# A written order for VectorE, ScalarE and GpSimd in an attention stage, with norms split in three, two widths of buffers and a later set-up

## The chip, the cores and the metric

The kernel runs on one core of one Trainium2 chip. The metric is the time of one execution on the device, in microseconds (us). Before the change three executions took 1590.54, 1592.66 and 1595.66 us; their median is 1592.66 us.

A core has these engines, each with an instruction queue of its own that is worked off in order: TensorE (PE in the profile; the loading of its weights is shown as PEld), VectorE (DVE), ScalarE (ACT), GpSimd (POOL) and SyncE (SP), which here only issues DMAs.

## The reference

The input is 32 sequences of 256 rows of 128 numbers. Two blocks follow each other, each as x = x + norm(block(norm(x))).

- The first block is a decoder layer: self-attention with a causal mask, cross-attention to one encoder sequence of 256 rows (the same for all 32), with an additive logit per key and a mask that lets a query see two keys past its own place, and an MLP with 512 hidden units and gelu. A layer norm stands ahead of each of the three, and a residual sum behind. There are 16 heads of 8 numbers.
- The second block is a mixture of experts: a shared expert and 8 routed ones of which the gate takes two, each a gated silu unit with 128 hidden units.

```python
q, k, v = split(layer_norm(h) @ c_attn_w + c_attn_b)
h = h + attend(q, k, v, causal) @ attn_proj_w + attn_proj_b
q = layer_norm(h) @ q_attn_w + q_attn_b
h = h + attend(q, k_enc, v_enc, scorer_logits, mask) @ x_proj_w + x_proj_b
h = h + gelu(layer_norm(h) @ fc_w + fc_b) @ mlp_proj_w + mlp_proj_b
x = x + norm(h)
x = x + norm(shared(norm(x)) + sum of two experts chosen per row)
```

## The kernel before, in words

**Stages.** The program has three stages: attention (lines 200 to 676), MLP with the choice of experts (lines 786 to 899), experts (lines 904 to 990). The change touches the first alone.

**One attention.** An object of class `Attention` is one sequence's self-attention (called S0 to S31 here) or cross-attention (X0 to X31). Its work is cut into pieces:

- `load` (line 350) brings 256 rows of x into one of five buffers. `normed_in` (line 361) takes means and variances on VectorE (`moments`, line 176), the power -1/2 on GpSimd (`rsqrt`, line 186: a `tensor_scalar` and a `pow` each), and writes normed rows on VectorE (`normed`, line 194). For a self-attention it does so twice: `xn`, which feeds the queries and keys, and `h_all`, the residual.
- `turned` (382) transposes `xn` on TensorE; `projections` (387) makes queries and keys, which ScalarE moves out of PSUM and GpSimd splits into three bf16 parts with four instructions (`projected`, lines 250 to 253: `qkp`). SP writes the parts to DRAM and reads them back in another layout (`load_queries`, line 262; `load_keys`, line 266). `values` (404) does the same for the values, without the detour.
- `maxima` (420) makes scores with queries on the partitions, and VectorE takes the row maxima, straight from PSUM (line 443). `split` (446) cuts these into three parts on GpSimd with five small instructions (`mparts`), `turned_maxima` (457) transposes them.
- `weights` (477) makes the scores once more with keys on the partitions, less the maxima, and ScalarE takes the exponential into SBUF buffers `wt` from the pool `wtp`, 22 buffers of 512 numbers (lines 502, 503).
- `weighted` (513) multiplies the weights with the values, for each half of the queries (line 525), ScalarE copies the result (`avs`). `back`, `turned_back` and `joined` (536 to 567) divide by the sums on VectorE, transpose and project, and VectorE adds to the residual.

**PSUM.** All that TensorE writes goes to 8 banks of 512 numbers, shared by all pieces (`bank`, line 161). A bank is free again when VectorE or ScalarE has read it.

**The order.** A planner (lines 584 to 649) gives each piece a step. Two steps make one pass of the loop at line 664. A pass issues the matmuls of up to two halves of maxima and two of weights, mixed (`issue`, line 569), then the reductions or exponentials that read them (`after`), and then the other pieces due at the two steps, `weighted` last. One self-attention takes 6 steps of maxima and one cross-attention 8, so from about step 96 on one sequence takes 14 steps, which is 7 passes.

The loop stands in a `manual_schedule` for TensorE (line 662): TensorE gets its instructions in the order of the program. For the other engines the framework's scheduler makes the order at build time, by its own estimate of durations, and it may move an instruction ahead as far as buffers allow. SP's order comes from it too, before the change and after it.

A norm is due 18 steps ahead of an attention's first scores, `turned` 14 steps ahead and `projections` 2 steps after that; a planner's budget may move them by 2.

**Set-up.** Constants are made by pieces of their own: `spares` and `diagonals` fill masks on GpSimd (lines 108 to 132), `max_frames` clears buffers on GpSimd (307), `picks`, `out_biases` and `logit_parts` work on VectorE (134 to 173), and `encoder_turned`, `encoder_rows`, `encoder_keys` and `encoder_values` (315 to 330) prepare the encoder's keys and values, which the first cross-attention uses at step 46. Before the change nearly all of it is due ahead of step 0 (lines 651 to 661).

Of the kernel before, what the change touches and what calls it, by code (L numbers as in the profile page):

```python
# [8 lines left out]
F32 = mybir.dt.float32  # L9
# [6 lines left out]
P = 128  # L16
# [8 lines left out]
EPS = 1e-5  # L25
# [19 lines left out]
def transformer_moe_kernel(ctx: ExitStack, tc: tile.TileContext, ins, out: bass.AP):  # L45
# [130 lines left out]
    def moments(pool, srcs, tag):  # L176

        n = len(srcs)
        st = pool.tile([P, n, 6], F32, tag=f"st{tag}", name="st")
        mv = pool.tile([P, n, 2], F32, tag=f"mv{tag}", name="mv")  # L180
        for i, s in enumerate(srcs):
            nc.vector.bn_stats(st[:, i, :], s)  # L182
            nc.vector.bn_aggr(mv[:, i, :], st[:, i, :])
        return mv

    def rsqrt(pool, mv, mul, add, tag):

        n = mv.shape[1]
        r = pool.tile([P, n], F32, tag=f"r{tag}", name="r")
        nc.gpsimd.tensor_scalar(r, mv[:, :, 1], mul, add, ALU.mult, ALU.add)  # L190
        nc.gpsimd.tensor_tensor(r, r, nhalf[:, 0:n], ALU.pow)  # L191
        return r

    def normed(dst, src, mv, r, i):
        nc.vector.tensor_scalar(dst, src, mv[:, i, 0:1], r[:, i : i + 1], ALU.subtract, ALU.mult)  # L195
# [4 lines left out]
    with ExitStack() as actx:  # L200
        wk = actx.enter_context(tc.tile_pool(name="wk", bufs=3))
        wl = actx.enter_context(tc.tile_pool(name="wl", bufs=5))
        wtp = actx.enter_context(tc.tile_pool(name="wtp", bufs=22))
        kx = actx.enter_context(tc.tile_pool(name="kx", bufs=1))
        dram = actx.enter_context(tc.tile_pool(name="dram", bufs=1, space=bass.MemoryType.DRAM))

# [135 lines left out]
        class Attention:  # L342
# [11 lines left out]
            def spares(self):  # L354
# [3 lines left out]
                if not self.cross:  # L358
                    fill_spare(k_rows[i], k_spare)

            def normed_in(self):
                self.xn = wk.tile([P, 2, D], F32, tag="xn", name="xn")
                if self.cross:
                    mv = moments(wk, self.hs, "a")
                    r = rsqrt(wk, mv, 1.0, EPS, "a")
                    for t in range(2):
                        normed(self.xn[:, t, :], self.hs[t], mv, r, t)
                else:

                    xs = [self.x[:, t, :] for t in range(2)]  # L370
                    mv = moments(wk, xs, "a")
                    r1 = rsqrt(wk, mv, 1.0, EPS, "a")
                    r2 = rsqrt(wk, mv, 1.0 + EPS, EPS * EPS, "b")
                    for t in range(2):
                        normed(self.xn[:, t, :], xs[t], mv, r2, t)
                        normed(self.hs[t], xs[t], mv, r1, t)

            def biased(self):
                h = h_all[:, 2 * self.b : 2 * self.b + 2, :]
# [97 lines left out]
            def weights(self, kb, js, gp):  # L477
                q0, nq = self.queries(kb)
                n = len(js)
                work, tiles = {}, []  # L480
                for g in (2 * gp, 2 * gp + 1):
                    st = slice(32 * g, 32 * g + 32)
                    t = bank("st")[:, 0 : n * nq]
                    t3 = t.rearrange("p (c q) -> p c q", q=nq)
                    tiles.append((g, t))
                    todo = []
                    for c, j in enumerate(js):
                        for part in range(3):
                            todo.append((nq, t3[:, c, :], self.kr[st, j, part, kb * P : kb * P + P],
                                         self.qs[st, j, q0:S], (c, part) == (0, 0)))  # L490
                        todo.append((nq, t3[:, c, :], pick[st, j, :], self.mT[st, q0:S], False))
                    for a in range(4):
                        at = 32 * a - (2 if self.cross and kb == 0 else 0)
                        skip = max(0, -at)
                        w = 32 - skip
                        todo.append((n * w, t3[:, :, at + skip : at + 32], eye[st, a, :],
                                     tri_k[st, skip:32].unsqueeze(1).to_broadcast([32, n, w]), False))
                    work[g] = todo

                def after():  # L500
                    for g, t in tiles:
                        w = wtp.tile([P, 512], F32, tag="wt", name="wt")
                        nc.scalar.activation(w[:, 0 : n * nq], t, AF.Exp)  # L503
                        for c, j in enumerate(js):
                            self.wts[kb, g, j] = w[:, c * nq : (c + 1) * nq]
                    self.done += 1
                    if self.done == len(self.key_halves()):
                        give(("qs", self.cross, self.b % QK_BUFS), self)
                        if not self.cross:
                            give(("kr", self.b % QK_BUFS), self)  # L510
                return work, after
# [75 lines left out]
        def on(step, f, *args):  # L587
            extra.setdefault(step, []).append((f, args))
# [15 lines left out]
        while ended < NB:  # L604
            ready = ended < begun and first[ended] <= at
            cross = begun == NB or (ready and not cross) or begun - ended == AHEAD
            if cross:
                x = pairs[ended][1]
                at = max(at, first[ended])
                ended += 1  # L610
            else:
                x = pairs[begun][0]
                begun += 1

            at = max(at, *(free.get((x.cross, what, x.b % n), at) for what, n in (("qk", QK_BUFS), ("v", V_BUFS))))
            at += at % 2
            halves, keys = x.query_halves(), x.key_halves()
            s = at
            at += len(halves)
            if not x.cross:  # L620
                on(s - 22, x.load)
            on(s - 18, x.normed_in)
            if x.b < QK_BUFS:
                on(s - 17, x.spares)
            on(s + 2, x.biased)
            e = full(s - 14, 0.35, x.turned)
            e = full(e + 2, 0.5 if x.cross else 0.9, x.projections)
            assert e <= s - 8, (e, s)
            if not x.cross:
                full(e + 2, 0.55, x.values)  # L630
            for i, h in enumerate(halves):
                by_query[s + i] = (x, h)
            for qb in range(2):
                last = s + max(i for i, h in enumerate(halves) if h[0] == qb)
                on(last + 1, x.split, qb)
                e = full(last + 3, 0.13, x.turned_maxima, qb)
                assert e < s + LAG
            for i, h in enumerate(keys):
                by_key[s + LAG + i] = (x, h)
            end = s + LAG + len(keys)  # L640
            free[x.cross, "qk", x.b % QK_BUFS] = end + 14
            half = end if x.cross else s + LAG + sum(h[0] == 0 for h in keys)
            e = full(half + 1, 1.2 if x.cross else 0.9, x.weighted, 0)
            e = full(max(e, end + 1), 1.8, x.weighted, 1)
            free[x.cross, "v", x.b % V_BUFS] = e + 12
            e = full(e + 2, 0.5, x.back)
            e = full(e + 2, 0.25, x.turned_back)
            e = full(e + 2, 0.6, x.joined)
            first[x.b] = e + 20

        on(-18, spares)
        on(-15, diagonals)
        on(-13, max_frames, False)
        on(-11, picks)
        on(-9, out_biases)
        full(-5, 0.5, encoder_turned)
        on(-5, logit_parts)
        on(-4, encoder_rows)
        full(-2, 0.5, encoder_keys)
        full(0, 0.5, encoder_values)  # L660
        on(2, max_frames, True)
        with tc.manual_schedule(engines={mybir.EngineType.PE}):
            s = min(extra) // 2 * 2 - 1
            while s <= max(extra):

                works = []
                for t in (s, s + 1):
                    works += [x.maxima(*h) for x, h in [by_query[t]]] if t in by_query else []
                    works += [x.weights(*h) for x, h in [by_key[t]]] if t in by_key else []
                issue(*[w for w, _ in works])  # L670
                for _, after in works:
                    after()
                for f, args in sorted(extra.get(s, []) + extra.get(s + 1, []),
                                      key=lambda e: e[0].__name__ == "weighted"):
                    f(*args)
                s += 2
# [109 lines left out]
    with ExitStack() as mctx:  # L786
        wk = mctx.enter_context(tc.tile_pool(name="wkm", bufs=3))
# [103 lines left out]
        E = mybir.EngineType  # L891
# [149 lines left out]
```

## Time and profile before

| | |
|---|---|
| time, median of three | 1592.66 us |
| time of the profiled execution | 1591.84 us |
| its span, first to last instruction | 1590.1 us |
| mean granted TensorE clock | 0.963 |
| busy: PE, DVE, ACT, POOL | 1407.4, 1054.3, 870.9, 653.1 us |
| attention | 0 to about 1015 us |
| MLP and choice | about 1015 to 1200 us |
| experts | about 1200 to 1590 us |

The span is 1.74 us shorter than the time of that execution. Busy time counts an engine as busy from the start to the end of each instruction; a busy TensorE needn't be at its peak, since matmuls overlap. An idle stretch of an engine is put down to the instruction that ended it: "PE av L525 <- DVE m L443" is TensorE waiting to start line 525, which writes `av`, until a reduction at line 443 was through. "Issue" stands for waits that the profile shows no cause of. PEclk is the share of TensorE's full clock that was granted.

### The profile page before, as it was taken

The numbers are of one execution on the slowest core, as the hardware profiler recorded it, in microseconds if no ns is written. First come the engines' busy times: TensorE is split into PE (matmuls) and PEld (weight loads), VectorE is DVE, ScalarE is ACT, GpSimd is POOL, SyncE is SP. The second block draws the span as 40 slices with busy tenths as digits, with TensorE's granted clock in tenths as the row PEclk, the third lists the DMA queues.
The fourth block names the chain that finished last, engine by engine and source line by source line (L and its number), as shares of the span: only waits on it lengthen the run. The fifth ranks groups of instructions, "written<-read, shape, count | busy, mean of one in ns | idle before, by whom it ended". The sixth has DMA issues, their size and how long they took to land.

```text
span 1590.1 us, 74601 instructions
## 1 busy us (share of the span) xinstructions
PE 1407.4 (89%) x32988; PEld 1099.7 (69%) x32988; DVE 1054.3 (66%) x2955; ACT 870.9 (55%) x2032; POOL 653.1 (41%) x1475
## 2 busy tenths in 40 slices
PE   3678898898988988888999899799979999999997
PEld 2566677776777777777777787478756666666664
DVE  5647667776677776677776666267866666666665
ACT  1353566665666666666666655677734443433433
POOL 7435445444445444444444322378631212222112
PEclk8788999999999999999999989899979999999998
DMA  5632223232232232232222200500000000000000
GB/s 140 189 99 79 65 91 101 65 115 77 71 115 73 91 100 66 84 103 64 93 89 82 66 16 28 148 20 1 1 1 8 7 14 14 8 14 14 7 14 14
DMA packets 106037, 97.27 MB, mean 61 GB/s; under 512 B 4764, under 2 KB 105360, under 8 KB 105712
## 3 DMA queue, kind: packets, MB, share of 16 engines
q1 hardware_dynamic: 104432, 91.49, 18.7%
q8 instruction: 258, 4.23, 1.1%
q10 hardware_dynamic: 1280, 1.01, 0.2%
q14 instruction: 67, 0.55, 0.1%
HBM read 54.47 MB, written 37.77 MB: 58 GB/s over the span
## 4 chain that ended last, share of the span: by engine, by line
PE 66%; DVE 18%; POOL 6%; ACT 4%; issue 3%; DMA 3%; SPq 0%; POOLq 0%; ACTq 0%; DVEq 0%
DVE m L443 11%; PE av L525 11%; PE sc L580 9%; PE po L940 8%; PE pa L929 8%; PE pb L930 8%; PE st L580 7%; PE po L844 4%; PE pf L837 3%; PE pq L245 2%; POOL r L191 2%; ACT wt L503 2%; DVE st L182 2%; PE pa L541 1%; DVE xn L195 1%
## 5 line engine op out<-in xcount | busy, mean ns | idle before, releaser
L443 DVE TENSOR_REDUCE m<-sc 128x2 f32<-128x512 f32 (+2 forms) x896 | 496.2, 607 | 236.8 <-PE sc L580 207.3
L503 ACT ACTIVATE wt<-st 128x512 f32<-128x512 f32 (+1 forms) x896 | 420.7, 539 | 261.1 <-PE st L580 199.8
L580 PEld LDWEIGHTS <-qs 32*128 32x128 bf16 x6144 | 226.4, 95 | 96.7 <-issue 83.5
L580 PE MATMUL st<-mT,pick 32*128 32x256 bf16 (+2 forms) x2048 | 242.7, 245 | 3.8 <-issue 3.7
L580 PEld LDWEIGHTS <-strips 32*128 32x128 bf16 x7424 | 190.2, 94 | 21.8 <-issue 18.4
L940 PEld LDWEIGHTS po<-w,h 128*128 128x128 f32 x1152 | 154.7, 191 | 67.9 <-issue 49.5
L580 PE MATMUL sc<-kr,qs 32*128 32x256 bf16 (+1 forms) x3072 | 165.6, 250 | 33.4 <-DMA kr<-k 24.7
L580 PE MATMUL st<-qs,kr 32*128 32x128 bf16 (+1 forms) x3072 | 179.3, 248 | 8.3 <-issue 4.8
L580 PE MATMUL st<-qs,krx 32*128 32x130 bf16 (+1 forms) x3072 | 177.6, 243 | 7.4 <-issue 5.6
L580 PE MATMUL sc<-krx,qs 32*128 32x256 bf16 (+1 forms) x3072 | 178.9, 246 | 5.6 <-issue 2.6
L934 DVE SCALAR_TENSOR_TENSOR h<-pb,cols,sa 128x512 f32<-128x512 f32 x144 | 107.9, 749 | 113.7 <-ACT sa L932 88.8
L932 ACT ACTIVATE sa<-pa,cols 128x512 f32<-128x512 f32 x144 | 99.7, 693 | 147.3 <-PE pa L929 120.4
L940 PE MATMUL po<-w,h 128*128 128x128 f32 x1152 | 161.9, 277 | 0.0
L929 PE MATMUL pa<-h_all,w 128*128 128x512 f32 x288 | 150.7, 605 | 0.0
L930 PE MATMUL pb<-h_all,w 128*128 128x512 f32 x288 | 147.9, 595 | 0.0
L580 PE MATMUL sc<-strips 32*128 32x64 bf16 (+2 forms) x3840 | 140.2, 193 | 6.5 <-issue 6.4
L580 PE MATMUL st<-strips 32*128 32x64 bf16 (+2 forms) x3584 | 137.2, 193 | 8.7 <-issue 8.6
L954 POOL TENSOR_TENSOR z<-z 128x512 f32<-128x512 f32 x32 | 40.7, 1271 | 245.9 <-ACT z L950 245.9
L525 PE MATMUL av<-wt,vpadx 128*32 128x128 f32 (+1 forms) x4096 | 111.5, 252 | 32.2 <-DVE m L443 28.6
L191 POOL TENSOR_TENSOR r<-r,nhalf 128x2 f32<-128x2 f32 (+1 forms) x160 | 133.0, 837 | 9.9
L580 PEld LDWEIGHTS <-kr 32*128 32x128 bf16 x3072 | 118.1, 95 | 16.7 <-issue 13.9
L525 PEld LDWEIGHTS av<-wt,vpadx 128*32 128x32 f32 x4096 | 97.8, 112 | 44.4 <-DVE m L443 36.6
(162 smaller groups left out, 2649.8 us busy)
## 6 DMA issues: line engine op xcount, KB each, us to landing
kr<-k SPq DMA_DIRECT2D x32, 768.0 KB
k<-qkp SPq DMA_DIRECT2D x32, 576.0 KB
qs<-q SPq DMA_DIRECT2D x64, 256.0 KB
q<-qkp SPq DMA_DIRECT2D x64, 192.0 KB
x<-in_x_dram SPq DMA_DIRECT2D x32, 128.0 KB
x_all<-in_x_dram SPq DMA_DIRECT2D x8, 512.0 KB
out_dram<-y SPq DMA_DIRECT2D x16, 256.0 KB
w<-in_rw_dram SPq DMA_DIRECT2D x1, 1024.0 KB
```

Of the source, the lines that this page charges most:

```text
L191: nc.gpsimd.tensor_tensor(r, r, nhalf[:, 0:n], ALU.pow)
L443: nc.vector.tensor_reduce(m[:, g, js[0] : js[0] + n], t3, AX.X, ALU.max, negate=True)
L503: nc.scalar.activation(w[:, 0 : n * nq], t, AF.Exp)
L525: nc.tensor.matmul(av[32 * g : 32 * g + 32, j // 2, to : to + n], lhsT=self.vp[:, kb, g, WINDOW[j] : WINDOW[j] + 32], rhs=self.wts[kb, g, ...
L580: nc.tensor.matmul(dst, lhsT=lhsT, rhs=rhs, start=start, stop=False, skip_group_check=True)
L837: nc.tensor.matmul(pf, lhsT=wfc[:, f * P : (f + 1) * P], rhs=self.xT, start=True, stop=True)
L844: nc.tensor.matmul(po[:, i, :], lhsT=self.g[:, f, i * P : (i + 1) * P], rhs=wmlp[:, f, :], start=f == 0, stop=f == FF // P - 1)
L929: nc.tensor.matmul(pa, lhsT=w1[:, e, 0:D], rhs=rhs, start=True, stop=True)
L930: nc.tensor.matmul(pb, lhsT=w1[:, e, D : 2 * D], rhs=rhs, start=True, stop=True)
L932: nc.scalar.activation(sa, pa, AF.Silu, bias=col(C_B1 + 2 * e))
L934: nc.vector.scalar_tensor_tensor(h, pb, col(C_B1 + 2 * e + 1), sa, ALU.add, ALU.mult)
L940: nc.tensor.matmul(po[:, i, :], lhsT=h[:, i * P : (i + 1) * P], rhs=w2[:, e, :], start=True, stop=e < NE)
```

## The change

The diff does four things.

- The `manual_schedule` around the attention loop now names PE, Activation, DVE and Pool. All four get their instructions in the order in which the program's loop makes them.
- `normed_in` becomes three pieces. `stats` (means, variances, powers) is due 20 steps ahead of the scores, `normed_in` (only `xn`) 17 ahead, and for a self-attention `normed_rows` (only `h_all`) 14 ahead. The power that `xn` needs is now the first one. `load` is due 26 steps ahead, where it was 22.
- The pool of exponentials has two kinds of buffers: 18 of 512 numbers and 8 of 260.
- The set-up is due later: `diagonals` at -11 (was -15), `picks` -9 (was -11), `max_frames` -7 and 14 (was -13 and 2), `out_biases` 1 (was -9), the encoder's pieces at 6 to 11 (were -5 to 0). `spares` alone is due earlier, at -21 (was -18).

No instruction is added or removed.

```diff
-        wtp = actx.enter_context(tc.tile_pool(name="wtp", bufs=22))
+        wtp = actx.enter_context(tc.tile_pool(name="wtp", bufs=1))
...
+            def stats(self):
+
+                srcs = self.hs if self.cross else [self.x[:, t, :] for t in range(2)]
+                self.mv = moments(wk, srcs, "a")
+                if self.cross:
+                    self.r = rsqrt(wk, self.mv, 1.0, EPS, "a")
+                else:
+                    self.r = rsqrt(wk, self.mv, 1.0 + EPS, EPS * EPS, "b")
+                    self.r1 = rsqrt(wk, self.mv, 1.0, EPS, "a")
+
             def normed_in(self):
                 self.xn = wk.tile([P, 2, D], F32, tag="xn", name="xn")
-                if self.cross:
-                    mv = moments(wk, self.hs, "a")
-                    r = rsqrt(wk, mv, 1.0, EPS, "a")
-                    for t in range(2):
-                        normed(self.xn[:, t, :], self.hs[t], mv, r, t)
-                else:
-
-                    xs = [self.x[:, t, :] for t in range(2)]
-                    mv = moments(wk, xs, "a")
-                    r1 = rsqrt(wk, mv, 1.0, EPS, "a")
-                    r2 = rsqrt(wk, mv, 1.0 + EPS, EPS * EPS, "b")
-                    for t in range(2):
-                        normed(self.xn[:, t, :], xs[t], mv, r2, t)
-                        normed(self.hs[t], xs[t], mv, r1, t)
+                for t in range(2):
+                    normed(self.xn[:, t, :], self.hs[t] if self.cross else self.x[:, t, :], self.mv, self.r, t)
+
+            def normed_rows(self):
+                for t in range(2):
+                    normed(self.hs[t], self.x[:, t, :], self.mv, self.r1, t)
...
-                        w = wtp.tile([P, 512], F32, tag="wt", name="wt")
+                        half = n * nq <= 260
+                        w = wtp.tile([P, 260 if half else 512], F32, tag=f"wt{int(half)}", name="wt",
+                                     bufs=8 if half else 18)
                         nc.scalar.activation(w[:, 0 : n * nq], t, AF.Exp)
...
             if not x.cross:
-                on(s - 22, x.load)
-            on(s - 18, x.normed_in)
+                on(s - 26, x.load)
+            on(s - 20, x.stats)
+            on(s - 17, x.normed_in)
+            if not x.cross:
+                on(s - 14, x.normed_rows)
...
-        on(-18, spares)
-        on(-15, diagonals)
-        on(-13, max_frames, False)
-        on(-11, picks)
-        on(-9, out_biases)
-        full(-5, 0.5, encoder_turned)
-        on(-5, logit_parts)
-        on(-4, encoder_rows)
-        full(-2, 0.5, encoder_keys)
-        full(0, 0.5, encoder_values)
-        on(2, max_frames, True)
-        with tc.manual_schedule(engines={mybir.EngineType.PE}):
+        on(-21, spares)
+        on(-11, diagonals)
+        on(-9, picks)
+        on(-7, max_frames, False)
+        on(1, out_biases)
+        full(6, 0.5, encoder_turned)
+        on(6, logit_parts)
+        on(7, encoder_rows)
+        full(9, 0.5, encoder_keys)
+        full(11, 0.5, encoder_values)
+        on(14, max_frames, True)
+        E = mybir.EngineType
+        with tc.manual_schedule(engines={E.PE, E.Activation, E.DVE, E.Pool}):
```

## The prediction

> **What bounds the kernel now.** I read first the busy time by stretches, cut where the stages change, since only attention is touched.
>
> ```profile
> core 0: us, PE busy (x) PEld busy (x) DVE busy (x) ACT busy (x) POOL busy (x), PEclk, DMA share, GB/s
> 0.00:34.40 34.40, 8.32 (x32) 5.94 (x33) 22.24 (x71) 6.06 (x14) 28.62 (x66) 0.87 0.48 127
> 34.40:64.00 29.60, 17.79 (x425) 14.85 (x428) 16.61 (x28) 5.25 (x16) 12.57 (x31) 0.74 0.74 221
> 64.00:205.00 141.00, 113.62 (x3561) 95.37 (x3553) 86.97 (x223) 73.09 (x171) 65.91 (x163) 0.88 0.28 84
> 205.00:960.00 755.00, 672.17 (x24510) 574.88 (x24500) 530.56 (x1317) 479.48 (x1166) 341.13 (x900) 0.99 0.26 83
> 960.00:1015.00 55.00, 48.43 (x1663) 39.74 (x1659) 27.02 (x85) 32.58 (x85) 10.83 (x41) 0.97 0.06 19
> ```
>
> TensorE is the bound in the steady part (205 to 960): 672 of 755 us busy, 83 idle. In the first 205 us it is idle for 65. So 148 us of 1590 can be won at the very most. The waits from 200 to 1000 us say who owns the 83:
>
> ```profile
> engine line waited for: us in total, times, longest us
> ...
> ACT wt L503 <- PE av L525: 37.9, 27, 2.1
> DVE h_all L195 <- POOL r L191: 37.8, 20, 1.9
> ...
> PE av L525 <- DVE m L443: 26.1, 40, 2.2
> PE st L580 <- issue: 22.5, 36, 2.5
> ...
> PE sc L580 <- issue: 11.6, 22, 1.2
> ...
> PE pt_x L211 <- DVE m L443: 7.8, 16, 2.0
> ```
>
> With the small rows (scores behind statistics 2.2 and 0.9, and m, a and pt_m rows of 1.7, 1.1, 0.8 and 0.4), VectorE holds TensorE up for 40.9 us; "issue" takes 37.4, and nothing in the diff touches it. One period (28.5 us, seven passes) shows how the 40.9 come about, in the timelines of VectorE, TensorE and ScalarE:
>
> ```profile
> 593.91 2.46 DVE L443 TENSOR_REDUCE m<-sc 128x2 f32<-128x512 f32 x4
> 596.29 0.59 DVE L195 TENSOR_SCALAR xn<-h_all,mv,r 128x128 f32<-128x128 f32 x2
> ...
> 599.05 0.60 DVE L195 TENSOR_SCALAR h_all<-x,mv,r 128x128 f32<-128x128 f32 x2 [1.89 <-POOL r L191]
> ```
>
> ```profile
> 600.31 0.96 PE L525 MATMUL av<-wt,vpadx 128*32 128x128 f32 x26 [1.30 <-DVE m L443]
> ```
>
> ```profile
> 601.03 1.09 ACT L503 ACTIVATE wt<-st 128x512 f32<-128x512 f32 x2 [1.68 <-PE av L525]
> ```
>
> The scheduler has packed both norms of a period between two rounds of reductions. VectorE reaches the self-attention's `h_all` before GpSimd has the power, stands for 1.89 us with four reductions queued behind it, and the banks that these would free are what TensorE's `av` lacks. ScalarE meanwhile lacks a buffer for exponentials. Put into passes, all such waits of TensorE from 245 to 880 us fall in these two of the seven passes: about 1.4 us a period.
>
> For the start I read the waits from 0 to 200 us; the largest of TensorE's is the keys' way through DRAM:
>
> ```profile
> PE sc L580 <- DMA kr<-k: 24.7, 4, 11.3
> ```
>
> **The change, part by part.**
>
> *Written order and moments ahead, steady part.* No instruction is added. In the written order GpSimd's power comes one whole pass or more ahead of VectorE's norm, so the 1.89 us stand goes. VectorE's work between the rounds of reductions shrinks too. Now it runs from 590.14 to 601.98 without a break but that stand: three rounds of four (2.4 each), 1.3 of join and statistics, then two norms, aggregates and two norms (1.4). Written out, the same three rounds have 0.96 (xn, join) and 1.2 (rows, statistics) between them: 9.4 us in place of 11.8. So TensorE's 1.30 and its shorter neighbours should mostly vanish. Of 40.9 us I take 80%: -33. What is late next? In these two passes TensorE itself, with its "issue" gaps. Elsewhere the keys: SP issues `kr<-k` for S28 at 792.64 and TensorE first uses it at 797.61, without a wait on record; over the steady part I find 5 to 8 us from issue to use, and 5.1 to 6.2 us is what the landings on the chain of waits take. So keys arrive just in time. The saved time lies almost wholly outside the five passes between projection and use, but VectorE may let the first scores start up to 0.6 us sooner (a wait of 0.59 at 593.33), and keys could eat that. I take off 5: **-28**. Ends: -41 (all of it), and 0 (the bank that `av` gets is freed by a reduction anyway).
>
> *Order on ScalarE and GpSimd.* Nearly free: ScalarE's trace already follows the program's order of exponentials and copies. On GpSimd the four instructions of `qkp` (3.7 us at 607.74) stand ahead of the next `split`; it ends at 612.78 and its transpose's copy starts at 615.19, so 2 us cover it. If that cover went, TensorE would pay the excess once a period.
>
> *Buffers.* By the plan of steps, when the last exponentials of a self-attention's first four halves come, 16 buffers of the cross-attention before and 8 of its own are held: 24 against 22. That is ScalarE's 37.9 us of waits for `av`. With two widths the most held in the steady part is 16 of 18 and 8 of 8, so they go. They are worth nothing by themselves (TensorE had its banks at 602.27 without a gap), but would be next. Price: in passes 27 and 61 of the start 20 wide ones are wanted, and ScalarE waits for one `av` (1.96 us) with the next copies queued behind; passes of slack cover it. 0, ends 0 and +4.
>
> *Set-up and start.* Before, S0's queries and keys leave ScalarE at 17.3, but GpSimd, busy with masks and with powers of S1 and S2, splits them from 20.74 to 25.04; the first scores start at 34.39. Written order: GpSimd's `spares` (3.8 us by rows at 5.67 to 12) end near 5.7, S0's first power at 6.7, `xn` 7.4 (before: 13.2), transposes and copy 9, projections 11.3, `qkp` 12.2 to 15.8. DRAM and back took 9.3 us (25.07 to 34.39): scores at 25, 9.6 earlier. Then come the costs. Passes -1 to 11 have two halves of maxima each, 2.4 us of VectorE per pass, so VectorE is the bound there (12.2 busy of 13.7 us from 39.3 to 53), and the moved steps now stand in its queue: `out_biases` 0.9, `logit_parts` 2.0, three value frames 3.9, S3's norms 1.2, in all 8 us, partly beside GpSimd's splits that TensorE waits for anyway. But S2's keys gain more: in the 7.95 us wait before 59.19 the split of S2's keys had waited until 43.38 behind a `split` of maxima; in the written order it is ahead of it, and they land near 42. And SP's 8.5 us wait of `kx<-parts` moves behind S2's keys. I work out pass 11's end at 51 to 52 (before 63.4): -11. S4's keys: GpSimd takes them at once (91.2, not 93.61 to 98.34 with powers and biases in between), -3.5 of the 4.93 us wait at 107.6. From 64 to 205 VectorE and GpSimd cause 19 us of waits above 0.3 us (4.38 at 175.07, 3.37 at 118.62, 2.51, 2.25 ...), of the steady part's kind; 40% of it: -8.
>
> *Clock.* The three stretches to 205 lose 0.13 x 2 x 34.4 + 0.26 x 2 x 29.6 + 0.12 x 2 x 141 = 58 us to half clock. [...] The rows say less: in these half-clock windows TensorE was busy for only 37 us, so 18 at most. Of them I count the 10 us window around the 7.95 us wait: -3.
>
> [...] The rows: one `xn` at 10.84 took 2.32 us, 6 of 64 over 0.5 (median 0.345), all in the start while GpSimd filled masks; but 64 cross norms took 0.333 us in the mean, none over 0.36, with GpSimd 45% busy beside them. I take the rows: +0.5 in the start, 0 later (ends 0 and +6).
>
> Sum: -28 - 11 - 3.5 - 8 - 3 + 0.5 = -53 from 1591.84: 1538.8 for this execution, and as the median stands 0.82 above it, **1540 us**. MLP and experts keep their 575 us.
>
> **Rivals.**
>
> *The start only.* `av`'s bank stays behind a reduction under any order, or the keys take the gain: 0 in the steady part, -25 in the start: 1567. For it: keys have next to no slack. Against: the wait sits right behind a stand that the order removes.
>
> *The steady part only.* The start is bound by VectorE and DMA (0.74 busy share of DMA from 34 to 64), and moved set-up gives back what the earlier scores gain: -28: 1564.
>
> *Slower: the keys' chain.* In place: between `projections` and the first scores five passes on. If in the written order GpSimd or SP takes up something else first (a `split` that waits for its reductions, an `x` load that waits for a buffer), keys land d later in each of some 28 periods. Price 28 x (d - 1); it outweighs -53 from d = 2.9 us on, and with one `qkp` of 3.7 ahead plus its wait of 2, d = 5.7, it gives 28 x 4.7 - 53 = +79: 1671. Against: nothing late stands ahead of `qkp` in its pass, and outside the start SP's waits for x buffers were 10.9 us in 14, none over 1.4.
>
> **How the numbers follow.** My forecast, -35 to -85: 0.65. The start only 0.12, the steady part only 0.11, the keys' chain 0.08, and 0.04 for gains and new waits that cancel. Faster by over 0.3% (about what a measurement of this kernel can tell from no change) 0.88, within it 0.04, slower 0.08. Low end: -41, -30 in the start, -12 of clock: 1510. High end: a third of the steady part's gain and nothing else sure: 1583.
>
> **What would show it.** Right: `h_all <- POOL r` and `wt <- PE av` gone from the steady waits; PE `av <- DVE m` under 10 us; a period near 27.4 us; first scores near 25 us; pass 11 near 52. Wrong: PE `sc <- DMA kr` in every period (keys), `av <- DVE m` unchanged (banks), or PE `pt_m <- POOL mparts` in every period (GpSimd's queue). My sum fails most easily in the start, where I chain estimates.

## The result and the profile after

The median of four runs is 1568.85 us (1567.22 to 1570.38), against 1592.36 us (1590.54 to 1595.66) for four runs of the kernel before. The ratio is 0.985, with a 95% interval of 0.9831 to 0.9869. That is 23.5 us faster, where the forecast was 52. The profiled execution took 1570.38 us with a span of 1568.7 us. The mean granted clock rose from 0.963 to 0.972.

The busy time by the same stretches, in the profile after:

```profile
0.00:34.40 34.40, 13.42 (x110) 10.10 (x110) 15.52 (x46) 6.17 (x14) 24.91 (x55) 1.00 0.65 183
34.40:64.00 29.60, 20.10 (x395) 15.46 (x399) 25.73 (x49) 6.29 (x19) 13.95 (x37) 0.71 0.61 177
64.00:205.00 141.00, 124.60 (x4072) 105.29 (x4064) 97.12 (x236) 83.13 (x196) 65.87 (x171) 0.92 0.31 96
205.00:960.00 755.00, 676.99 (x24718) 576.42 (x24722) 544.80 (x1342) 484.84 (x1174) 343.90 (x916) 1.00 0.26 80
```

From 64 to 205 us TensorE does 4072 matmuls where it did 3561. In the steady part it does only 208 more in 755 us (24718 against 24510), under 1%. So the gain is in the start, and the steady part, from which the forecast drew 28 us, gave next to nothing. Yet the waits that were to go have gone. The waits from 200 to 1000 us, after:

```profile
engine line waited for: us in total, times, longest us
...
PE st L584 <- issue: 28.8, 42, 2.1
...
PE av L529 <- issue: 15.0, 19, 1.6
...
PE sc L584 <- DVE h_all L569: 11.7, 19, 1.1
PE sc L584 <- issue: 11.6, 23, 1.4
...
PE sc L584 <- DMA kr<-k: 3.1, 4, 1.4
```

No row for `h_all <- POOL r` (37.8 us before) and none for `wt <- PE av` (37.9 us) is left. TensorE's `av <- DVE m`, 26.1 us before, has no row left either; with waits too short for a row it comes to 1.8 us. But `st <- issue` has grown from 22.5 to 28.8, and a row for `av <- issue` stands there with 15.0 us (2.7 before). With short waits counted, the waits of TensorE from 205 to 945 us that VectorE ends fell from about 43 to 16 us; those put down to "issue" rose from 37 to 53.

Most of VectorE's remaining 16 us is the new row `sc <- DVE h_all`. In one of the two passes that the forecast named, `xn` (0.94 us) and the residual sum (0.41 us) now stand between two rounds of reductions, and TensorE waits there for 0.57 us a period, where it waited for 0.53 us before. So of the two waits only the one for `av`, 0.90 us a period, really went.

Steps of the start and of the steady part, from the ends of the row maxima of single passes in the traces (a period is the time from pass 97 to pass 391, divided by its 21 periods):

| us | before | after | forecast for after |
|---|---|---|---|
| first scores | 34.39 | 26.56 | 25 |
| end of pass 11 | 63.40 | 59.58 | 51 to 52 |
| end of pass 45 | 138.63 | 127.61 | |
| end of pass 97 | 252.94 | 234.36 | |
| end of pass 391 | 860.99 | 838.66 | |
| end of pass 461 | 992.58 | 969.51 | |
| one period | 28.95 | 28.78 | 27.4 |

By pass 97 the kernel after is 18.6 us ahead, and the 21 periods that follow add only 3.7. These are figures of single executions. In kernels of the experiments below that have the same start as the kernel after, the first scores come between 25.1 and 27.4 us and pass 11 ends between 57.9 and 59.7; in those that have its order in the steady part (after, e2, e4, e8), the period lies between 28.54 and 28.91 us. So the steady part gained somewhere between nothing and 0.4 us a period, far from the 1.1 us that -28 asks for.

**Where the steady gain went.** One of the passes in which the forecast put the gain did get shorter by nearly the forecast amount, from 5.55 to 4.22 us in the mean (from 250 to 860 us, by the ends of the maxima). The next pass got longer, from 4.03 to 5.28 us, and TensorE's delays without a cause in it rose from 0.35 to 1.18 us. The other five hardly moved. What these waits are can be seen in TensorE's timeline of the kernel after (start, duration, what it does; in brackets the idle time ahead and what ended it):

```profile
367.83 0.26 PE L584 MATMUL sc<-krx,qs 32*128 32x256 bf16 x1 [0.32 <-issue]
...
371.79 0.36 PE L529 MATMUL av<-wt,vpadx 128*32 128x2 f32 x21 [0.22 <-issue]
...
376.08 1.83 PE L529 MATMUL av<-wt,vpadx 128*32 128x128 f32 x57 [1.60 <-issue]
...
379.83 0.23 PE L584 MATMUL st<-strips 32*128 32x128 bf16 x1 [0.70 <-issue]
```

Four stops, at `sc`, `av`, `av` and `st`, some 4 us apart, in the midst of runs of the same instruction. Counted through TensorE's stream (weight loads and matmuls together), they are instructions 19905, 20161, 20417 and 20673: each is 256 behind the one before. From 205 to 945 us, 60 of the 64 starts that lacked a cause for over 0.4 us in the kernel before stand at this one place modulo 256, and 81 of 86 in the kernel after. All delays over 0.3 us there come to 53.5 us before and 75.5 us after. The profile's DMA queues say what comes in such portions:

```profile
q8 instruction: 258, 4.23, 1.1%
```

258 packets with 4.23 MB for TensorE's 65976 instructions: that comes to 256 instructions a packet, with 64 bytes each. (The kernel e7 below has 8192 instructions fewer and 226 packets, 32 fewer.) In the trace, the packet for the next block starts about 1.1 us after TensorE has entered a block and takes about 1.1 us. At each stop one has just landed, and TensorE goes on some 1.3 to 1.5 us later. So a block of 256 seldom takes much under 3.5 us here, even where its own work needs less: from 205 to 945 us one in ten takes less than 3.44. In the kernel after, the blocks that end in a stop do their own work in a median of 2.97 us; of those that don't, three in four take 3.55 us or more. I call this the **supply** theory: a wait inside a block that would else be under the floor costs nothing, and taking it away puts a wait for instructions in its place. What goes beyond the floor is not covered. The rivals are that VectorE is still the bound, that TensorE's array is, or that the late set-up gives the gain back.

### The profile page after: what moved, and what is told of

Same layout as the page of the kernel before. It is cut to its first block, busy times and chain, and to the rows that moved or that the text cites. A ratio compares the mean times of both kernels' runs of the same rounds, so it can differ in the third digit from the quotient of the medians.

```text
span 1568.7 us, 74300 instructions
## 1 busy us (share of the span) xinstructions
PE 1410.2 (90%) x32988; PEld 1099.5 (70%) x32988; DVE 1068.4 (68%) x2955; ACT 872.9 (56%) x2032; POOL 648.5 (41%) x1475
## 3 DMA queue, kind: packets, MB, share of 16 engines
q8 instruction: 258, 4.23, 1.1%
## 4 chain that ended last, share of the span: by engine, by line
PE 73%; DVE 11%; issue 5%; DMA 5%; ACT 4%; POOL 2%; SPq 0%; POOLq 0%; ACTq 0%; DVEq 0%
PE av L529 12%; PE sc L584 11%; PE st L584 9%; PE po L948 8%; PE pa L937 8%; PE pb L938 8%; DVE m L445 7%; PE po L852 4%; PE pf L845 3%; PE pq L245 3%; ACT wt L507 2%; DMA kr<-k 2%; PE pa L545 1%; DMA k<-qkp 1%; DVE xn L195 1%
## 5 line engine op out<-in xcount | busy, mean ns | idle before, releaser
L584 PE MATMUL st<-mT,pick 32*128 32x256 bf16 (+2 forms) x2048 | 239.0, 243 | 2.8 <-issue 2.8
L584 PE MATMUL sc<-kr,qs 32*128 32x256 bf16 (+1 forms) x3072 | 169.9, 252 | 37.1 <-DMA kr<-k 15.3
L190 POOL TENSOR_SCALAR r<-mv 128x2 f32<-128x2 f32 (+1 forms) x160 | 31.3, 196 | 262.1 <-DVE mv L183 231.3
```

Source lines behind the costliest of these rows:

```text
L584: nc.tensor.matmul(dst, lhsT=lhsT, rhs=rhs, start=start, stop=False, skip_group_check=True)
```

## The experiments

All times are medians, and each ratio is to the kernel before on the same chip (1590.74 us for the first four kernels, 1595.71 for the next four, 1597.99 for the last four). A ratio without an interval is from one execution. "Stops" are TensorE's delays over 0.3 us at the one place modulo 256, "DVE" its idle time ended by VectorE, both in us per period of the profiled execution.

| kernel | time | ratio (95%) | pass 11 | pass 97 | period | DVE | stops |
|---|---|---|---|---|---|---|---|
| before | 1592.36 | 1 | 63.4 | 252.9 | 28.95 | 1.56 | 2.24 |
| after | 1568.85 | 0.985 (0.9831 to 0.9869) | 59.6 | 234.4 | 28.78 | 0.67 | 2.82 |
| e1 scheduler's order | 1615.4 | 1.0157 (1.0118 to 1.0196) | 60.8 | 257.4 | 29.83 | 2.12 | 1.67 |
| e2 set-up early | 1563.76 | 0.9832 (0.9793 to 0.9871) | 59.2 | 236.5 | 28.54 | 0.73 | 2.54 |
| e3 norms together | 1706.21 | 1.0724 (1.0682 to 1.0767) | 68.7 | 273.4 | 33.01 | 4.53 | 1.46 |
| e4 one width | 1563.78 | 0.982 (0.9769 to 0.987) | 58.7 | 237.0 | 28.62 | 0.68 | 2.76 |
| e5 light VectorE | 1560.47 | 0.978 | 53.9 | 227.1 | 28.92 | 0.11 | 3.84 |
| e6 half columns | 1568.14 | 0.983 | 57.9 | 233.6 | 28.66 | 0.96 | 4.14 |
| e7 two parts | 1496.16 | 0.938 | 59.7 | 224.2 | 26.56 | 1.05 | 1.22 |
| e8 is e2 and e4 | 1572.52 | 0.9844 (0.9812 to 0.9876) | 60.1 | 239.9 | 28.91 | 0.64 | 3.10 |
| e9 no key DMAs | 1539.04 | 0.963 | 58.5 | 224.6 | 27.91 | 1.11 | 1.62 |
| e10 before, two parts | 1543.88 | 0.9667 (0.9639 to 0.9696) | 64.0 | 248.0 | 27.24 | 2.21 | 0.75 |
| e11 is e7 again | 1496.22 | 0.9367 (0.9338 to 0.9397) | 58.1 | 224.7 | 26.64 | 1.17 | 0.96 |
| e12 frames early | 1488.37 | 0.9327 (0.9291 to 0.9363) | 53.0 | 217.2 | 26.52 | 1.02 | 0.98 |

### Undoing one part of the change at a time

**e1, the scheduler's order again.** The kernel after, with only TensorE's order written out:

```diff
-        with tc.manual_schedule(engines={E.PE, E.Activation, E.DVE, E.Pool}):
+        with tc.manual_schedule(engines={mybir.EngineType.PE}):
```

> The changed kernel with the written order for TensorE alone; VectorE, ScalarE and GpSimd are ordered by the scheduler again. Theory (TensorE's instructions arrive in blocks of 256, and a block can't be worked off in less than about 3.5 us, so in the steady part a wait on VectorE and a wait for instructions stand in for each other): the period stays within 0.2 us of the changed kernel's 28.57 us, and what changes is the start, where the order is what brought the first scores forward: 1575 to 1590 us. Rival (the steady part did gain from the order and lost it again to new waits of the order): the period is longer or shorter by over 0.5 us, and the time moves by over 13 us from that alone.

It came out at 1615.4 us, slower than before the change. The supply theory missed here, and the rival's marks were met: the period was to stay within 0.2 us and grew by 1.05. The other three parts of the change are worth nothing without the written order; with them in, the order is worth some 47 us. Its waits from 240 to 820 us:

```profile
DVE h_all L195 <- POOL r L191: 48.6, 19, 2.6
...
PE av L529 <- DVE m L445: 34.6, 35, 2.4
```

The stand of VectorE for GpSimd's power, and with it TensorE's wait, is back, and larger than in the kernel before (35.9 and 22.3 us in the same window). TensorE's waits for VectorE rose by 1.45 us a period and the stops fell by 1.15. The granted clock may be part of what is left: it was 0.96 from 240 to 820 us, where the kernel after had 1.00. Powers that are due earlier don't take the stand away; the order in which the scheduler puts them does the harm.

**e2, set-up as early as before; e4, one width of buffers; e8, both.**

```diff
-        on(-21, spares)
-        on(-11, diagonals)
...
+        on(-18, spares)
+        on(-15, diagonals)
...
-                        w = wtp.tile([P, 260 if half else 512], F32, tag=f"wt{int(half)}", name="wt",
-                                     bufs=8 if half else 18)
+                        w = wtp.tile([P, 512], F32, tag="wt", name="wt", bufs=22)
```

> The changed kernel with the set-up due at its old steps (before the first scores), everything else as changed. If the later set-up brings the start its gain, the first scores come at 32 us or later instead of 26.6, and the time is 1574 to 1580 us. Rival (the moved set-up stands in VectorE's queue between the first reductions and gives back what the earlier scores gain): first scores later, but pass 11 ends no later than the changed kernel's 59.6 us, and the time is 1562 to 1570 us.

> The changed kernel with 22 buffers of 512 for the exponentials instead of two widths. ScalarE's waits for buffers (37.9 us before) come back. Theory: not on TensorE's path, 1567 to 1573 us. Rival (the buffers were the part of the change that let the steady part go): period up by over 0.5 us, 1582 us or more.

> The changed kernel with the set-up at its old steps and one width of 22 buffers: the written order and the norms in three steps alone. Both undone parts by themselves gave 1563.8 us; if each is worth its 5 us, this run takes 1557 to 1562 us; if they only differ by noise from the changed kernel, 1563 to 1570 us.

The three ratios, 0.9832, 0.982 and 0.9844, have intervals that all hold 0.985, though e4's and e8's times lie a few us outside the ranges that were expected. Neither part has a worth that these runs can measure. In e4 ScalarE's waits for `av` are back (21.6 us from 200 to 1000 us), and cost nothing. With the early set-up the first scores come 4 us later (30.71 against 26.56), but pass 11 ends at 59.2 against 59.6: what the later set-up gives to the first scores is taken back before pass 11.

**e3, the three pieces of the norm due at one step again**, in the written order:

```diff
-                on(s - 26, x.load)
-            on(s - 20, x.stats)
-            on(s - 17, x.normed_in)
+                on(s - 22, x.load)
+            on(s - 18, x.stats)
+            on(s - 18, x.normed_in)
...
-                on(s - 14, x.normed_rows)
+                on(s - 18, x.normed_rows)
```

> The changed kernel with moments, xn and rows all due at 18 steps ahead, and the load at 22, as before the change. VectorE now waits for GpSimd's power in its written order, some 2 us or more twice a period. Theory (instruction blocks): waits of TensorE on VectorE come back and its waits without a shown cause shrink by about as much; the period grows by less than 0.7 us and the time is 1569 to 1588 us. Rival (VectorE sets the pace of the steady part): two stands of 2 us in each of 27 periods add 50 us or more: 1615 us and up.

At 1706.21 us it is far beyond what the supply theory allowed, and on the rival's side (1615 us and up). Its waits from 240 to 820 us:

```profile
PE sc L584 <- DVE m L445: 70.6, 34, 4.3
DVE xn L195 <- POOL r L191: 67.1, 35, 2.8
...
PE st L584 <- issue: 9.8, 16, 1.2
```

VectorE now meets the missing power in each norm with all its reductions queued behind, and nothing may be moved past. So the order and the three steps of lead only work together. It also says how little the supply of instructions covers here: TensorE's waits for VectorE rose by 3.9 us a period and the stops fell by only 1.4. I had taken the cover to be larger. That leaves 2.5, but the period grew by 4.2. Part of the rest is probably the clock: from 240 to 820 us TensorE stood at half clock for 92 us (granted 0.92), against 3.4 us in the kernel after (1.00). In the kernel after, the matmuls of line 852 that follow each other without a gap start 213 ns apart at half clock (median of 24) and 112 ns apart at full clock (median of 471). If all of the 92 us were work at half speed, it would cost 46 us, or an estimated 2.6 us a period at most.

### What bounds the steady part

**e5, VectorE's reductions over half of each row.** This leaves out half of the work on the maxima; the exponential's argument is scaled down so that it stays finite.

```diff
-     nc.vector.tensor_reduce(m[:, g, js[0] : js[0] + n], t3, AX.X, ALU.max, negate=True)
+     nc.vector.tensor_reduce(m[:, g, js[0] : js[0] + n], t3[:, :, 0 : nk // 2], AX.X, ALU.max, negate=True)
```

> The changed kernel with VectorE's maxima taken over the first half of the columns only, and the exponent scaled by 0.01 so that it stays finite: this leaves out half of the maxima's work (VectorE's reductions fall from 497 to about 300 us). Theory (instruction blocks of TensorE): what TensorE waits for VectorE in the steady part (0.67 us a period) goes, and of that at most half reaches the period: 28.3 to 28.8 us against 28.78. Rival (VectorE still sets the pace through the banks that it frees): the period falls below 27.5 us.

**e6, half of the columns in two of three parts of each product of keys and queries**, with the same instructions (shown for the maxima; the weights likewise):

```diff
-     todo = [(nk, t3[:, c, :], self.qs[st, j, qb * P : qb * P + P], self.kr[st, j, part, 0:nk],
+     todo = [(nk, t3[:, c, 0 : nk // (1 if part == 0 else 2)], self.qs[st, j, qb * P : qb * P + P],
+              self.kr[st, j, part, 0 : nk // (1 if part == 0 else 2)],
```

> The changed kernel with the second and third part of each key-query product on half of the columns: part of the scores is left out, as many instructions as before, a third fewer columns in these products. Theory (instruction blocks): TensorE's array is not what paces the dense passes; the period falls by less than 1.5 us (to 27.3 us or more), and the stalls at block ends grow from 2.8 us a period to 4 us or more. Rival (the array is the pace): a third of the columns of about 18 us of key products in a period goes, and the period falls to 25 us or less, as in the next run.

**e7, the third part of the keys left out**, in the maxima and in the weights: as many columns as e6, but 4096 matmuls and 4096 loads fewer.

```diff
-  (c, part) == (0, 0)) for c, j in enumerate(js) for part in range(3)]
+  (c, part) == (0, 0)) for c, j in enumerate(js) for part in range(2)]
...
-                        for part in range(3):
+                        for part in range(2):
```

> The changed kernel with two parts of the keys instead of three in the key-query products: the same number of columns as the run with half columns, but 4096 matmuls and as many weight loads fewer (8192 of 65976 instructions of TensorE). Theory (instruction blocks): the period falls with the number of instructions, by some 14%, to 24 to 26 us, clearly below the run with half columns. Rival (the array): the same period as with half columns, within 0.5 us.

e5 took VectorE's waits away almost wholly (0.11 us a period), and the period didn't shorten (28.92 against 28.78, just above the range expected): the stops grew by 1.0 us instead. Its waits from 240 to 820 us:

```profile
PE st L584 <- issue: 21.0, 31, 1.4
PE sc L584 <- issue: 16.6, 23, 1.6
PE av L529 <- issue: 14.8, 17, 1.6
```

Then e6 against the kernel after, each from 240 to 840 us; the first row is of the kernel after, the second of e6:

```profile
240.00:840.00 600.00, 539.11 (x19607) 459.74 (x19599) 440.36 (x1082) 388.45 (x936) 287.58 (x756) 1.00 0.28 88
```

```profile
240.00:840.00 600.00, 501.68 (x19677) 415.31 (x19663) 439.99 (x1084) 387.23 (x938) 287.54 (x755) 0.99 0.29 88
```

TensorE is busy for 37 us less, and does 70 matmuls more in 600 us. Its array isn't the bound, and the stops took what was saved (4.14 us a period). e7, with the same columns as e6 and 13% fewer instructions in a period (1629, not 1882), has a period of 26.56 us and takes 1496 us. So the number of instructions is what the time follows. The period was to fall to 24 to 26, so it follows by less than its full share: with 1.22 us of stops left, VectorE's 1.05 and waits for keys (15.7 us in 580), other things are again nearly as late.

**e9, no queries and keys through DRAM from the fifth sequence on**: these use the parts of the first four sequences, which leaves out their own. The instructions stay; the DMA share falls from 0.28 to 0.03.

```diff
-                load_queries(self.qs, dq)
-                load_keys(self.kr, k_rows[i])
+                if self.b < QK_BUFS:
+                    load_queries(self.qs, dq)
+                    load_keys(self.kr, k_rows[i])
```

> The changed kernel without the DMAs of queries and keys from the fifth sequence on: later sequences use the queries and keys of the first four; this leaves out moving 57 MB, all other work stays. If the instruction blocks come late because they queue behind these DMAs, the stalls at block ends (2.8 us a period) fall below 1.4 us and the period below 27.6 us. If their time is fixed whatever the DMA engines carry, stalls and period stay within 0.4 us (28.4 to 29.2 us).

The stops fell from 2.82 to 1.62 us and the period from 28.78 to 27.91, between the two expectations. So a part of the stops, near half, goes with the data's DMAs, and the rest doesn't. In the mean, an instruction packet from 205 to 945 us starts 0.95 us after its block is entered, where it started after 1.16, and takes 1.08 us, where it took 1.12. So it is the start that is earlier, which fits a packet that stands behind others; that it stands behind the keys' is not shown. Its waits from 240 to 820 us:

```profile
PE sc L588 <- issue: 10.1, 15, 1.2
PE st L588 <- issue: 6.6, 12, 0.9
...
PE av L533 <- issue: 3.3, 10, 0.5
```

**e10 and e11, the same change with fewer instructions.** If the supply had swallowed the gain, the change should be worth more when TensorE has fewer instructions. e10 is the kernel before with e7's edit; e11 is e7 with intervals.

> The kernel before the change with two parts of the keys instead of three (the third part's products are left out): 8192 instructions of TensorE fewer. Beside the next run it shows what the change is worth when TensorE is less short of instructions. Theory: the waits on VectorE, which the supply of instructions covered, now count, so the change's forecast gain returns: this kernel's period is longer than 26.56 us by 0.8 us or more, and its time is 45 us or more above the changed kernel with two parts (1540 us or more where that one takes 1496). Rival (the written order gives the steady part nothing, whatever TensorE waits for): the periods differ by 0.2 us as they do with three parts, and the times by 20 to 27 us, from the start alone.

> The changed kernel with two parts of the keys, as in the look before, timed against the kernel before: 1490 to 1502 us, a ratio of 0.935 to 0.945, with a period of 26.4 to 26.8 us.

It is: 1543.88 to 1496.22 us is 47.7 us or 3.1%, twice the 23.5 us or 1.5% with all instructions, and the intervals of the two ratios are far apart. e10's waits from 240 to 820 us show the forecast's picture, with little of "issue" in it:

```profile
PE av L525 <- DVE m L443: 31.5, 51, 2.2
...
PE st L580 <- issue: 5.6, 7, 1.6
```

In the profiled executions the period falls by 0.60 us (27.24 to 26.64) where it fell by 0.18. That is three times as much, but under the 0.8 expected, and with single executions differing by some 0.4 us a period the factor is not sharp. VectorE's waits fell by 1.04 us between the two, so 0.4 of that is again lost. Waits for keys take 0.16 of it (`sc <- DMA kr`, 11.0 us in e11, 7.6 in e10), stops 0.2. By pass 97 the profiled executions differ by 23.3 us (18.6 with all instructions), and from there to pass 461 by another 16.0 (4.5). They differ by 37.2 us in all, less than the medians do, because e10's is its fastest; where the other 10 us are made is not known.

### The start

**e12, VectorE's set-up ahead of the first maxima.** On top of e7's edit, the value frames are cleared at steps -23 to -9 and no longer within `values`; `out_biases` and `logit_parts` come before step 0.

```diff
+        on(-23, value_frame, v_pads[0])
+        on(-17, value_frame, v_pads[1])
+        on(-11, value_frame, v_pads[2])
+        on(-11, value_frame, v_pads[3])
+        on(-9, value_frame, v_cross)
-        on(1, out_biases)
+        on(-7, out_biases)
-        on(6, logit_parts)
+        on(-5, logit_parts)
```

> The changed kernel with two parts of the keys and with VectorE's part of the set-up (value frames, out_biases, logit_parts) due ahead of the first scores again; GpSimd's and the encoder's stay late. If VectorE's moved set-up is what gave back the earlier first scores by pass 11, pass 11 ends near 54 us (59.7 with it late) and the time is 4 to 7 us below the run before it; if not, within 3 us of it.

Pass 11 ends at 53.0 us against 58.1 in e11, as the queue of VectorE says it should. This is VectorE's timeline in the kernel after:

```profile
45.73 0.27 DVE L137 TENSOR_SCALAR left<-rows 1x256 f32<-1x256 f32 x1
46.04 0.72 DVE L139 CAST parts<-left 1x256 bf16<-1x256 f32 x1
46.79 1.33 DVE L141 TENSOR_TENSOR left<-left,parts 1x256 f32<-1x256 f32 x1
48.16 0.58 DVE L139 CAST parts<-left 1x256 bf16<-1x256 f32 x1
48.77 1.33 DVE L141 TENSOR_TENSOR left<-left,parts 1x256 f32<-1x256 f32 x1
50.14 0.70 DVE L139 CAST parts<-left 1x256 bf16<-1x256 f32 x1
50.76 2.47 DVE L445 TENSOR_REDUCE m<-sc 128x4 f32<-128x512 f32 x4
```

Six instructions on a single partition take 5.1 us in one piece, between reductions that TensorE's banks wait for:

```profile
51.49 1.44 PE L584 MATMUL sc<-kr,qs 32*128 32x256 bf16 x21 [4.42 <-DVE m L445]
```

They are slow where GpSimd splits queries and keys at the same time:

```profile
46.70 1.15 POOL L251 TENSOR_TENSOR qk<-qk,qkp 128x512 f32<-128x512 f32 x1
...
48.68 1.15 POOL L253 TENSOR_TENSOR qkp<-qk,qkp 128x512 bf16<-128x512 f32 x1
```

VectorE's two instructions at line 141 take 1.33 us each beside these and end 0.3 us after them. Over all kernels here, 16 of the 28 such instructions took 1.33 us, each beside one of GpSimd's at line 251 or 253; 11 stood beside none and took 0.35 to 0.42 us (both of e12's among them), and one that met only the beginning of one took 0.71. So GpSimd is the likely cause; no run was made to test it.

e5, whose reductions are half as long, also reaches pass 11 early, at 53.9. e12's median is 7.9 us below e11's, but the intervals of the ratios (0.9291 to 0.9363, and 0.9338 to 0.9397) overlap. e12 is the fastest of the kernels here; it leaves out the third part of the keys, so it is no version of the whole computation.

## Why the prediction was right in sign and wrong in size

- **The local signs were right.** VectorE's stand of 1.89 us, ScalarE's waits for buffers and TensorE's for `av` went, as the sum had it, and no wait for keys or for `pt_m` came in each period. The order with its three steps of lead did that: e1 without the order and e3 without the lead both bring the stand back. VectorE's wait in the other of the two passes only changed its instruction.
- **The steady term, -28, was the step that failed; measured, -3.7 over 21 of its some 26 periods, and not told apart from nothing.** The failing words are "TensorE itself, with its 'issue' gaps", "'issue' takes 37.4, and nothing in the diff touches it". I named the next limit and then let it stand as a constant. It is no constant: behind it stands a floor under each block of 256 instructions (one in ten took less than 3.44 us), and the stops grew when another wait inside the block went. VectorE's part of TensorE's idle time fell by 0.89 us a period (1.56 to 0.67), the stops rose by 0.58 (2.24 to 2.82), and 0.18 was left as gain. Of the remaining 0.13, waits for keys took 0.10. e5 shows the same exchange once more, e6 rules out the array, and e7, e10 and e11 show that fewer instructions bring more of the gain out. e1 and e3 show the limit: waits that come in addition are covered only in part (the stops fell by 1.15 us a period for 1.45 us of VectorE's waits in e1, by 1.4 for 3.9 in e3).
- **The start's first term, -11 at pass 11, measured -3.8.** The first scores came 7.8 us earlier (forecast 9.6). S2's keys no longer make TensorE wait, as forecast, but VectorE does in their place (4.42 us). `logit_parts`, put at 2.0 us, took 5.1, and in `out_biases` VectorE waits for TensorE twice for 0.9 us. e12 gets 5.1 us of it back. I sized these from instructions of the kernel before (0.4 us for the `tensor_tensor` that took 1.33 here), where GpSimd filled masks beside them. So the term for set-up beside GpSimd, +0.5, was too small as well: `xn` was looked at, but not the instructions that were being moved next to `qkp`. The end of +6 beside it is shown by no run: in the kernel after, two instructions took 1.33 us each beside GpSimd, where they took 0.40 in the kernel before.
- **The rest of the start came out in its sum, in part by luck.** From pass 11 to pass 97 the kernel gains a further 14.8 us, where the terms for S4's keys, for the waits from 64 to 205 us and for the clock were -3.5, -8 and -3, together -14.5. But the traces show other shares. TensorE's waits above 0.3 us that VectorE and GpSimd cause from 64 to 205 us fell from 19.1 to 6.3 us, by more than forecast. Its waits for keys there rose from 5.4 to 6.7: S4's fell only from 4.93 to 3.24, and a new one of 3.48 stands at 169.1. The clock term doesn't belong here, and failed: the half-clock window around the 7.95 us wait (10.24 us from 53.0 on) has one of the same length in its place from 49.1 on. That a wait of TensorE sets the granted clock, which the -3 and the -12 of the low end take for granted, is shown by no run: in the place of the 7.95 us wait stands one of 4.42 us, with 10.24 us at half clock as before. TensorE was busy for only 4.0 us of the first, so by the prediction's own reckoning it was worth 2 us at most. What did change is the clock later on: from 64 to 205 us the time at half clock fell from 34 to 24 us (granted 0.88 and 0.92), which no term of the sum had counted.
- **Buffers and set-up, put at 0 and at gains of the start:** e2, e4 and e8 give both nothing measurable. For the buffers that is what the sum said. For the set-up it isn't: the 4 us at the first scores are real, but VectorE's queue takes them back.
- **The rivals.** The time fell where "the start only" stood (1567 us), though not for its reason: neither the bank nor the keys held the steady part. The slower case didn't come; from 200 us on keys made TensorE wait for 3.1 us in four places.
- **What stays open.** e7 and e10 take away the instructions' supply and their execution at once, so how much of their gain is the one and how much the other is not told apart; e9 gives the first alone, in part. A kernel whose instructions are as many but arrive sooner wasn't tried.

## What to carry to other kernels

Before a wait is counted as gain, look at what its engine would be doing next: if gaps without a cause stand at a constant count of instructions (here 81 of 86 at one place modulo 256), the engine may be living on its supply of instructions, and time taken from another wait may come back there (here the stops grew by 0.58 us a period as its waits for VectorE fell by 0.89). In this kernel fewer instructions paid, and a better order or less work per instruction paid little: one third fewer columns in the score products gave next to nothing (a ratio of 0.983 after 0.985), and 13% fewer instructions in a period brought it to 0.937. A hand-written order needs its producers well ahead, since in it nothing is moved past a wait (in e3 VectorE stood for 67.1 us of 580 ahead of `xn`): here the same order gave -1.5% with three steps of lead and +7.2% without. And work that is moved should be priced beside its new neighbours: two instructions of 0.4 us took 1.33 each here.

## What the runs showed of the hardware

TensorE's instructions came in blocks of 256 with 16 KB each (258 packets, 4.23 MB). In the kernel after, the blocks that stop took a median of 3.75 us, and nine in ten of them 3.46 us or more, where their own work took 2.97. The stops come to 75.5 of 740 us. So the arrival of the next block wasn't hidden here, where pairs of a short load and a short matmul ran at some 12 ns per instruction (2.97 us for 256). Without the keys' DMAs (DMA share 0.03 instead of 0.28) the stops fell from 2.82 to 1.62 us a period.

A small instruction of VectorE with two operands (1x256 numbers) took 1.33 us beside a GpSimd `tensor_tensor` of 128x512, in 16 of 16 cases, and 0.35 to 0.42 us in the 11 cases away from it.
